# Sum of two tables and relu in one VectorE instruction: the first layer of a position bias

## The chip, the cores and the metric

The kernel runs on one core of one Trainium2 chip. The metric is the device time of one execution in microseconds (us). The engines are TensorE (PE in the profile; its weight loads are PEld), VectorE (DVE), ScalarE (ACT), GpSimd (POOL) and SyncE (SP). Executions of one kernel agreed within some 0.2% here.

## The reference, cut to what matters

The program is a sequence of four layers on an input of 2 x 512 x 32 x 32. The first is an attention with sampled keys whose scores get a bias from a small network of three layers on the distance of query and key:

```python
pos = grid_q[:, :, None, :] - grid_kv[:, None, :, :]
bias = jnp.sign(pos) * jnp.log1p(jnp.abs(pos))
bias = jax.nn.relu(bias @ cpb_w1 + cpb_b1)      # the layer that is changed
bias = jax.nn.relu(bias @ cpb_w2 + cpb_b2)
bias = (bias @ cpb_w3 + cpb_b3).reshape(...)
sim = jnp.einsum('bhid,bhjd->bhij', qh, kh) + bias
# ... softmax, values, projection, an MLP, and three more attention layers (cut)
```

The distance has an x part and a y part, so the first layer is the sum of one table over 32 columns and one over 32 rows, then a relu.

## The kernel before

A *unit* is one tile of 128 hidden channels by 1024 queries for one key. There are 1024 units. `first` makes the first layer on VectorE (in one unit of four, "quad 3", the relu is on ScalarE), `second` multiplies by the 128 x 128 weights on TensorE and evicts `z` from PSUM with ScalarE, `third` adds four units into `sim`.

```python
h1p = l0.enter_context(tc.tile_pool(name="att_h1", bufs=4))
ps_z = l0.enter_context(tc.tile_pool(name="att_ps_z", bufs=3, space=PSUM))
# ... (cut)
def first(u):
    # ... loads of the tables (cut)
    h1 = h1p.tile([P, H, W], F32, name="h1")
    nc.vector.tensor_tensor(                                       # L359
        h1,
        tx[:, quad, ri, :].unsqueeze(1).to_broadcast([P, H, W]),
        ty[:, quad, ri, :].unsqueeze(2).to_broadcast([P, H, W]),
        ALU.add,
    )
    h1f = h1.rearrange("p y x -> p (y x)")
    if quad == 3:
        nc.scalar.activation(h1f, h1f, AF.Relu)                    # L367
    else:
        nc.vector.tensor_scalar(h1f, h1f, 0.0, None, ALU.max)      # L369
    return h1f

def second(h1f):
    z = zt([P, HW], "z")
    for half in range(2):
        n = slice(half * HALF, (half + 1) * HALF)
        nc.tensor.matmul(z[:, n], cpb_w2, h1f[:, n], start=True, stop=True)   # L376
    h2 = h2p.tile([P, HW], F32, name="h2")
    nc.scalar.activation(h2, z, AF.Relu, bias=col("cpb_b2"))       # L378
    return h2
# ... (cut)
AHEAD = 2
for u in range(AHEAD):
    ready[u] = first(u)
for u in range(units + 2):
    if u + AHEAD < units:
        ready[u + AHEAD] = first(u + AHEAD)
    if u < units:
        h2s[u] = second(ready.pop(u))
    if u % 3 == 2:
        next(behind, None)      # one step of the work of other head pairs: offsets, samples, softmax
    # ... every eighth unit: third() for two rows, at the end of a head pair its scores (cut)
```

A step of `behind` on VectorE stands behind the sums of the units up to u + 2, and before all later ones.

## Time and profile before

| | before |
|---|---|
| median | 4073.86 us (4071.02 to 4075.19, 4 runs) |
| granted clock of TensorE | 0.991 |
| stage of the position bias | 84 to 2499 us of the span of 4073.9 |
| in that stage busy | TensorE 2371.6, VectorE 1910.8, ScalarE 1455.9 us |
| TensorE idle just before `z` | 43.4 us |

A group's line gives engine, operation, output<-input and the count, then busy time and the mean length of one, then the engine's idle time just before them and who ended it. The first thing to read is that TensorE is busy for 98% of the stage and VectorE for 79% (the weight loads, busy for 40%, 964 us, do not show how full TensorE is); the second is how little of TensorE's idle time stands before `z`. The lines themselves stand in the prediction below.

### The profile page before, as it was taken

How to read it: one execution, taken by the hardware profiler on the slowest of the kernel's cores; microseconds unless marked ns; L12 is line 12 of the kernel's file. 1: busy time of each engine (PE TensorE's matmuls, PEld its weight loads, DVE VectorE, ACT ScalarE, POOL GpSimd, SP SyncE). 2: the span in 40 equal slices, each digit the busy share in tenths (PEclk: the TensorE clock that was granted, in tenths of full speed). 3: DMA queues.
4: the chain of work that ended last, by engine and by line, in shares of the span. 5: the costliest groups of instructions: out<-in, count | busy, mean ns of one | idle time of the engine just before them, and what ended most of it. 6: DMA issues, size and time to landing. Idle time of an engine off the chain costs nothing.

```text
span 4073.9 us, 33014 instructions
## 1 busy us (share of the span) xinstructions
PE 3957.9 (97%) x13114; PEld 1627.1 (40%) x13114; DVE 2330.7 (57%) x2566; ACT 1767.5 (43%) x1843; POOL 264.5 (6%) x176
## 2 busy tenths in 40 slices
PE   6999999999999999999999998999999999999999
PEld 4343344343343343343343433444433333444443
DVE  3877877877877777877877774000016436230222
ACT  2665666665665466665656653111114324101011
POOL 0000110110010000010010010000000000000000
PEclk8999999999999999999999999999999999999999
DMA  3000101000011000000000000100010000000000
GB/s 110 21 16 11 22 16 54 20 16 16 16 16 16 11 16 16 16 21 11 22 16 13 19 16 0 52 8 11 8 49 1 1 0 1 13 0 0 0 21 22
DMA packets 95726, 72.87 MB, mean 18 GB/s; under 512 B 10576, under 2 KB 84688, under 8 KB 95056
## 3 DMA queue, kind: packets, MB, share of 16 engines
q1 hardware_dynamic: 92736, 69.18, 6.5%
q8 instruction: 108, 1.77, 0.2%
q10 hardware_dynamic: 2832, 1.51, 0.1%
q14 instruction: 50, 0.41, 0.0%
HBM read 62.03 MB, written 8.65 MB: 17 GB/s over the span
## 4 chain that ended last, share of the span: by engine, by line
PE 87%; DVE 10%; ACT 2%; issue 1%; DMA 0%; POOL 0%; ACTq 0%; SPq 0%; DVEq 0%; POOLq 0%
PE z L376 36%; PE sim L385 10%; PE pw L135 5%; PE ph L835 5%; PE pp L844 5%; PE pm L865 4%; DVE h L359 4%; PE pmv L135 4%; PE score L950 3%; PE pv L997 3%; PE score L135 3%; DVE acc L226 2%; DVE h L369 2%; PE pp L135 1%; PE ppr L890 1%
## 5 line engine op out<-in xcount | busy, mean ns | idle before, releaser
L376 PE MATMUL z<-h,cpb_w 128*128 128x512 f32 x4096 | 1818.8, 598 | 43.4 <-DVE h L369 28.3
L378 ACT ACTIVATE h<-z,pc 128x1024 f32<-128x1024 f32 x1024 | 1132.4, 1110 | 784.6 <-PE z L376 782.0
L359 DVE TENSOR_TENSOR h<-tab,tab 128x1024 f32<-128x1024 f32 x1024 | 1252.1, 1231 | 313.1 <-PE z L376 310.8
L376 PEld LDWEIGHTS z<-h,cpb_w 128*128 128x128 f32 x4096 | 760.8, 190 | 1065.4 <-issue 966.1
L369 DVE TENSOR_SCALAR h<-h 128x1024 f32<-128x1024 f32 x768 | 560.8, 730 | 26.3
L385 PE MATMUL sim<-h,w 128*32 128x512 f32 x4096 | 466.0, 595 | 0.0
L367 ACT ACTIVATE h<-h 128x1024 f32<-128x1024 f32 x256 | 269.3, 1052 | 131.7 <-DVE h L359 131.1
L345 POOL TENSOR_SCALAR tab<-tab,pc 128x512 f32<-128x512 f32 x64 | 120.4, 1882 | 2170.2 <-DMA tab<-slog_d 1469.3
L385 PEld LDWEIGHTS sim<-h,w 128*32 128x32 f32 x4096 | 120.2, 110 | 320.8 <-issue 320.2
L951 ACT ACTIVATE p<-score 128x1024 f32<-128x1024 f32 x144 | 139.5, 1020 | 212.4 <-PE score L950 210.0
L847 DVE SCALAR_TENSOR_TENSOR x<-pp,pc,x 128x512 f32<-128x512 f32 x16 | 12.0, 751 | 375.7 <-PE pp L844 375.7
L135 PE MATMUL pw<-p,vT 128*128 128x512 f32 x512 | 222.9, 597 | 1.3 <-DVE y L1049 1.3
L835 PE MATMUL ph<-xn,wa 128*128 128x512 f32 x512 | 220.9, 593 | 1.4 <-POOL xn L819 1.4
L844 PE MATMUL pp<-hid,wb 128*128 128x512 f32 x512 | 220.4, 592 | 0.0
L901 DVE TENSOR_TENSOR acc<-acc,p 128x2048 f32<-128x2048 f32 x56 | 129.7, 2316 | 133.2 <-ACT p L951 86.0
L838 ACT ACTIVATE hid<-ph,pc 128x512 f32<-128x512 f32 x64 | 44.0, 687 | 332.6 <-PE ph L835 332.6
L135 PEld LDWEIGHTS pw<-p,vT 128*128 128x128 f32 x512 | 97.8, 191 | 123.5 <-issue 122.0
L835 PEld LDWEIGHTS ph<-xn,wa 128*128 128x128 f32 x512 | 97.2, 190 | 123.1 <-issue 120.4
L844 PEld LDWEIGHTS pp<-hid,wb 128*128 128x128 f32 x512 | 97.4, 190 | 122.3 <-issue 122.3
L865 PE MATMUL pm<-hc,wa 128*128 128x512 f32 x256 | 128.5, 629 | 6.2 <-DMA wa<-in_qkv_w 6.2
L950 PE MATMUL score<-q,k 64*128 64x512 f32 x512 | 127.2, 615 | 0.0
L997 PE MATMUL pv<-p,vT 128*64 128x512 f32 x512 | 123.8, 605 | 0.0
(191 smaller groups left out, 1981.9 us busy)
## 6 DMA issues: line engine op xcount, KB each, us to landing
tab<-slog_d SPq DMA_DIRECT2D x128, 256.0 KB, 6.0
wa<-in_qkv_w SPq DMA_DIRECT2D x8, 768.0 KB, 7.4
x<-in_x SPq DMA_DIRECT2D x8, 512.0 KB, 5.2
xt<-in_xt SPq DMA_DIRECT2D x8, 512.0 KB, 4.0
wa<-in_mlp_w SPq DMA_DIRECT2D x4, 1024.0 KB, 15.8
wb<-in_mlp_w SPq DMA_DIRECT2D x16, 256.0 KB, 5.4
x_d<-x SPq DMA_DIRECT2D x16, 256.0 KB, 2.0
out<-x SPq DMA_DIRECT2D x16, 256.0 KB, 2.0
```

The costliest lines, as they stand in the source:

```text
L135: nc.tensor.matmul(pm, w, m, start=(k == 0), stop=(k == len(pairs) - 1))
L359: nc.vector.tensor_tensor(h1, tx[:, quad, ri, :].unsqueeze(1).to_broadcast([P, H, W]), ty[:, quad, ri, :].unsqueeze(2).to_broadcast([P, H, ...
L367: nc.scalar.activation(h1f, h1f, AF.Relu)
L369: nc.vector.tensor_scalar(h1f, h1f, 0.0, None, ALU.max)
L376: nc.tensor.matmul(z[:, n], cpb_w2, h1f[:, n], start=True, stop=True)
L378: nc.scalar.activation(h2, z, AF.Relu, bias=col("cpb_b2"))
L385: nc.tensor.matmul(sim[quad * 32 : quad * 32 + 32, n], w3[:, 31 - r : 63 - r], h2s[quad][:, n], start=(r == 0), stop=False,)
L835: nc.tensor.matmul(ph, w1[:, k, m * P : (m + 1) * P], xn_now[:, k, :], start=(k == 0), stop=(k == CC - 1))
L844: nc.tensor.matmul(pp, w2[:, k, m * P : (m + 1) * P], h1[:, k, :], start=(k == 0), stop=(k == HID // P - 1))
L865: nc.tensor.matmul(pm, w[:, k, cols], h[k][:, n], start=(k == 0), stop=(k == CC - 1))
L950: nc.tensor.matmul(sc[:, part, :], k[r, left[part]], q[r, n], start=True, stop=True)
L997: nc.tensor.matmul(pv[part * 64 : part * 64 + 64, n], vT[:, ls, lo : lo + 64], lp[:, part, n], start=(ls == 0), stop=(ls == 7),)
```

## The change

The two VectorE instructions become one custom instruction, `TENSOR_ADD_SAT`. By its definition in the library that the kernel imports it from it adds two inputs, takes the minimum with a first scalar and the maximum with a second. With the largest float and zero it is a sum and a relu. The intent is to spare 768 instructions on VectorE and 256 on ScalarE.

```diff
-            nc.vector.tensor_tensor(
-                h1,
-                tx[:, quad, ri, :].unsqueeze(1).to_broadcast([P, H, W]),
-                ty[:, quad, ri, :].unsqueeze(2).to_broadcast([P, H, W]),
-                ALU.add,
+
+            nc.vector._custom_dve(
+                TENSOR_ADD_SAT,
+                out=h1,
+                in0=tx[:, quad, ri, :].unsqueeze(1).to_broadcast([P, H, W]),
+                in1=ty[:, quad, ri, :].unsqueeze(2).to_broadcast([P, H, W]),
+                s0=float(np.finfo(np.float32).max),
+                s1=0.0,
             )
-            h1f = h1.rearrange("p y x -> p (y x)")
-            if quad == 3:
-                nc.scalar.activation(h1f, h1f, AF.Relu)
-            else:
-                nc.vector.tensor_scalar(h1f, h1f, 0.0, None, ALU.max)
-            return h1f
+            return h1.rearrange("p y x -> p (y x)")
```

(An import is cut.)

More of the change, by code (lines that the diff above doesn't have):

```diff
@@ L9 @@
 from concourse._compat import with_exitstack
+from concourse.dve_ops import TENSOR_ADD_SAT
 F32 = mybir.dt.float32
```

## The prediction

> **What bounds the kernel now.** I read the page first (busy shares, slices, chain of waits), then the waits of TensorE alone in the stage of the position bias, then the stage's timeline around those waits.
>
> ```profile
> PE 3957.9 (97%) x13114; PEld 1627.1 (40%) x13114; DVE 2330.7 (57%) x2566; ACT 1767.5 (43%) x1843; POOL 264.5 (6%) x176
> ...
> PE   6999999999999999999999998999999999999999
> DVE  3877877877877777877877774000016436230222
> PEclk8999999999999999999999999999999999999999
> ...
> L376 PE MATMUL z<-h,cpb_w 128*128 128x512 f32 x4096 | 1818.8, 598 | 43.4 <-DVE h L369 28.3
> L378 ACT ACTIVATE h<-z,pc 128x1024 f32<-128x1024 f32 x1024 | 1132.4, 1110 | 784.6 <-PE z L376 782.0
> L359 DVE TENSOR_TENSOR h<-tab,tab 128x1024 f32<-128x1024 f32 x1024 | 1252.1, 1231 | 313.1 <-PE z L376 310.8
> L369 DVE TENSOR_SCALAR h<-h 128x1024 f32<-128x1024 f32 x768 | 560.8, 730 | 26.3
> L367 ACT ACTIVATE h<-h 128x1024 f32<-128x1024 f32 x256 | 269.3, 1052 | 131.7 <-DVE h L359 131.1
> ```
>
> TensorE is busy nearly everywhere and its clock is full; VectorE is at seven to eight tenths in the first 25 slices and itself waits 310.8 us there for TensorE to give back a buffer. The changed lines (L359, L369, L367) lie in that stage alone, which runs from 84 to 2499 us. All that TensorE waits for in it:
>
> ```profile
> PE z L376 <- DVE h L369: 28.3, 24, 2.4
> PE z L376 <- ACT h L367: 9.6, 18, 1.4
> PE z L376 <- ACT h L378: 5.3, 5, 1.2
> ```
>
> That is 43.2 us in 47 waits. The chain of waits, in order of time, shows what an undisturbed stretch looks like:
>
> ```profile
> 311.03 13.93 PE z L376 x32
> 328.53 13.93 PE z L376 x32
> 346.03 13.93 PE z L376 x32
> ```
>
> One period of 8 units (32 passes of z and the sim passes between) takes 17.50 us with no wait. The stage has 1024 units, so 128 periods: 128 x 17.50 = 2240 us. The stage is 2499 - 84 = 2415 us. The other TensorE work in it (offsets, samples, scores, transposes, projection) has some 130 us by the busy column of its groups, and 2240 + 130 + 43 = 2413: the account closes, so outside those 47 waits TensorE is the bound and VectorE's speed buys nothing.
>
> A waiting matmul loses a little more than the idle time shown. A pass is recorded as 593 ns, but in a row passes start 429 ns apart (16 passes in 6.87 us), so a break also loses the overlap of some 0.16 us: 47 x 0.16 = 7.7 us. **The ceiling of the change is thus 43 + 8 = 51 us, 1.25% of 4072.8.**
>
> Where the waits come from is seen in the timeline at a change of head pair:
>
> ```profile
> 1286.53 1.22 DVE L415 TENSOR_REDUCE mx<-pt 128x16 f32<-128x1024 f32 x1 [6.91 <-PE pt L412]
> ...
> 1287.79 1.22 DVE L418 TENSOR_TENSOR at<-pt,mx 128x1024 f32<-128x1024 f32 x1
> 1288.93 1.22 DVE L359 TENSOR_TENSOR h<-tab,tab 128x1024 f32<-128x1024 f32 x1
> ...
> 1290.18 0.69 DVE L369 TENSOR_SCALAR h<-h 128x1024 f32<-128x1024 f32 x1
> ...
> 1291.02 1.96 PE L376 MATMUL z<-h,cpb_w 128*128 128x512 f32 x4 [1.09 <-DVE h L369]
> ```
>
> VectorE first has to wait for TensorE's transposes, then does two softmax operations, and only then makes the next unit; the two units made ahead are used up and TensorE stands for 1.09 us. The relu is the last 0.7 us ahead of the matmul.
>
> [...] No trace so far holds such a custom instruction[...].
>
> **The change part by part.**
> - VectorE: 1024 tensor_tensor (1252.1 us) become 1024 fused instructions[...]. 768 tensor_scalar (560.8 us) go. VectorE busy: 2331 - 561 = 1770 us, 43%. In a row an add and its relu take 1.86 us from start to start (1288.93 to 1290.79), an add alone 1.14 us (1287.79 to 1288.93); so a unit of three of the four quads costs VectorE 0.72 us less.
> - ScalarE: 256 relus (269.3 us) go: 1767 - 269 = 1498 us, 37%. The fourth quad also loses a hop from VectorE to ScalarE and its place in ScalarE's queue, where it stood between the evictions of z.
> - TensorE: the same matmuls, nothing added. No buffer, transfer or byte is changed.
> Most of the 830 us removed lies beside TensorE. What counts is each of the 47 waits, which I went through in the timeline, in four kinds:
> 1. Head-pair changes with the softmax on VectorE. Five of the seven show waits of about 1.1, 0.2 and 1.6 us, 14.6 us in all. After: the first unit is ready 0.7 us sooner, which leaves 0.36. For the later one, from 1288.93: three units 3 x 1.14, a sum 1.25, a reciprocal 0.29, a product 1.14, then the unit's own 1.25 and 0.12 for the signal: ready at 1296.4. TensorE would ask for it at about 1295.7; 0.7 us stay. About 1.0 of 2.9 us each: 5 us stay. The other two changes show one wait of 1.36 us on the ScalarE relu; 0.36 each stays, 0.7 in all.
> 2. The sample weights (a 1.15 us operation that waits for ScalarE): five waits, 6.7 us. Each is shortened by 0.7 to 0.8: 2.7 us stay.
> 3. The offset taps (six instructions, 2.16 us) and the small sample products: waits of 0.2 to 1.3 us. VectorE is behind there only because it had worked without a break for several units at 1.86 us each; at 1.14 it would have caught up. Nothing stays. The waits behind ScalarE's table loads (about 1 us) go with the 1.05 us relu that stood in the same queue.
> 4. The first unit of all: 2.40 us, of which 0.7 goes: 1.7 stays.
> Sum that stays: 5 + 0.7 + 2.7 + 1.7 = 10 us; I add 2 for waits that I can't foresee: 12. Saved idle: 43 - 12 = 31. Of the 47 breaks some 18 to 20 stay, so 27 to 29 times 0.16 us comes on top: 4.5. Saved in all about 36 us: **4072.8 - 36 = 4037 us, 0.9% faster.**
>
> **The rivals.**
> - A slow custom instruction. If the two further steps or the dispatch of the program cost time, VectorE loses the gain: the average unit now takes (3 x 1.86 + 1.14)/4 = 1.68 us of it, so at some 1.75 us per instruction the change is a wash on VectorE and only ScalarE's part is won (4050 to 4070). TensorE asks for a unit every 17.50/8 = 2.19 us; beyond 2.2 us an instruction, VectorE with its other work would be the bound, and a loss of 2% would come. [...] I take 5% for over 1.6 us.
> - TensorE is busy anyway and the waits move elsewhere: on ScalarE's evictions of z (three PSUM buffers), or on VectorE's softmax. The weight loads already wait 58.1 us for the evictions at L378, though hardly any of that reaches a matmul (5.3 us). If half the waits come back this way, the time is about 4055. Against it: ScalarE is at 6 tenths and loses a fifth of its work in the stage.
> - A large gain, read off the chain of waits, which gives VectorE 10% of the span (L359 4%, L369 2%), or off 830 us of removed work: 100 us or more, under 3970. Against it is the ceiling of 51 us; the chain walks through VectorE while TensorE is fed from units made ahead.
> - All waits go: 4022.
>
> **Range and chances.** The centre is 4037; the low end, 4024, is nearly the ceiling, the high end, 4054, the case of half the waits coming back or a somewhat slower instruction. Over 2% faster needs 81 us, above the ceiling: 1%. Over 2% slower needs the very slow instruction: 2%. Within 2%: 97%.
>
> **What would show it.** Right: the fused group at 1.2 to 1.25 us x1024, VectorE near 1770 and ScalarE near 1498 us busy, TensorE's idle before z at 8 to 16 us, its releaser mostly VectorE at head-pair changes and at the sample weights, the rest of the kernel from 2499 us on as long as before. Wrong: a fused instruction over 1.4 us; idle before z still over 25 us; a period of other than 17.50 us in undisturbed stretches; or a granted clock that falls when TensorE stands less.

The forecast's sum: it came to 31 + 4.5, about 36 us saved, and 4072.8 - 36 = 4037 us. The forecast takes the fused instruction to last as long as the add does in the trace before (median 1219 ns, starts 1.14 us apart); that was the assumption and no trace had shown it. The chance of 5% for over 1.6 us is an estimate without other support.

## The result, and the profile after

The changed kernel took 4034.27 us (4031.47 to 4037.9, 4 runs) against 4073.86. The ratio is 0.9904 with an interval of 0.9887 to 0.9921. The granted clock was 0.991 in the profiled run of either. The result was correct.

Of the page of the changed kernel: busy times, VectorE's slices, the groups of the stage. L361 is the fused instruction, L375 `z`, L377 its eviction.

```profile
PE 3949.7 (98%) x13114; PEld 1629.2 (40%) x13114; DVE 1809.8 (45%) x1798; ACT 1546.7 (38%) x1587; POOL 211.7 (5%) x176
...
DVE  2655655655655655655655552000016446130222
...
L375 PE MATMUL z<-h,cpb_w 128*128 128x512 f32 x4096 | 1810.3, 597 | 10.9 <-DVE h L361 10.3
L361 DVE CUSTOM_DVE_ANT_1 h<-tab,tab 128x1024 f32<-128x1024 f32 x1024 | 1242.9, 1230 | 784.9 <-PE z L375 784.1
L377 ACT ACTIVATE h<-z,pc 128x1024 f32<-128x1024 f32 x1024 | 1138.8, 1114 | 1095.6 <-PE z L375 1095.4
```

The fused instruction has a mean of 1230 ns, the add had 1231. VectorE now waits 784 us for TensorE to give back a buffer, against 311: it has nearly half a millisecond more to spare, and nearly all of it went into waiting. TensorE's idle time before `z` went from 43.4 to 10.9 us.

The stage in one window each, before and after (window, its length, then busy time of each engine with its count of instructions, granted clock, share of the DMA engines, GB/s):

```profile
84.00:2499.00 2415.00, 2371.63 (x8803) 964.10 (x8802) 1910.76 (x2166) 1455.85 (x1443) 216.67 (x124) 1.00 0.08 18
```

```profile
84.00:2458.00 2374.00, 2363.35 (x8803) 967.08 (x8804) 1390.98 (x1398) 1234.62 (x1186) 163.10 (x124) 1.00 0.08 18
```

The whole gain lies in this stage: what follows it took 1575 us before and 1576 after. In undisturbed stretches a period still takes 17.50 us, as the chain of waits of the changed kernel shows:

```profile
256.10 13.93 PE z L375 x32
270.03 3.57 PE sim L384 x32
273.60 13.93 PE z L375 x32
```

The waits that are left at a change of head pair, in the timeline of the changed kernel:

```profile
1267.60 1.23 DVE L417 TENSOR_TENSOR at<-pt,mx 128x1024 f32<-128x1024 f32 x1
1268.74 3.49 DVE L361 CUSTOM_DVE_ANT_1 h<-tab,tab 128x1024 f32<-128x1024 f32 x3
...
1270.10 5.39 PE L375 MATMUL z<-h,cpb_w 128*128 128x512 f32 x12 [0.36 <-DVE h L361]
...
1273.68 1.22 DVE L423 TENSOR_TENSOR at<-at,sm 128x1024 f32<-128x1024 f32 x1
...
1274.82 4.62 DVE L361 CUSTOM_DVE_ANT_1 h<-tab,tab 128x1024 f32<-128x1024 f32 x4
1276.19 1.95 PE L375 MATMUL z<-h,cpb_w 128*128 128x512 f32 x4 [0.70 <-DVE h L361]
```

The two waits of 0.36 and 0.70 us stand where the kernel before had 1.09, 0.18 and 1.70 (at 1291.02, 1293.15 and 1298.55 us of its trace): VectorE still does its softmax ahead of the next unit, but each unit comes 0.7 us sooner.

**A second way to count.** A pass of TensorE that comes a little late shows no idle time, because the recorded pass is longer (593 ns) than the distance to the next one (429), so a break loses up to some 0.16 us (593 - 429) that no idle column shows; before, 51 breaks are 50.4 us by starts and 43.4 us of idle time. So I also took the starts of the matmuls from the trace and summed what lies over 429 ns between a pass of `z` and the next pass of `z` (and the few breaks between side work and `z`). Over 170 ns I call it a break, from 20 to 170 ns a short delay.

| kernel | median us | ratio to before | idle before z | breaks: count, us | short delays, us |
|---|---|---|---|---|---|
| before | 4073.9 | 1 | 43.4 | 51, 50.4 | 20.8 |
| changed | 4034.3 | 0.9904 | 10.9 | 28, 15.1 | 15.5 |
| quads 0 to 2 fused | 4040.8 | 0.9916 | 16.7 | 31, 21.3 | 16.6 |
| quad 3 fused | 4068.0 | 0.9982 | 36.1 | 42, 42.6 | 19.5 |
| changed, 3 ahead | 4018.2 | 0.9860 | 2.0 | 6, 2.7 | 13.8 |
| before, 3 ahead | 4055.0 | 0.9950 | 23.0 | 48, 31.9 | 18.0 |
| quad 3 fused, 3 ahead | 4034.0 | 0.9904 | 14.4 | 20, 16.3 | 15.9 |
| a clamp more | 4102.1 | 1.0069 | 58.1 | 58, 68.8 | 24.9 |
| fused twice | 4381.4 | 1.0753 | 233.0 | 452, 319.6 | 44.2 |

From before to changed, breaks give 50.4 - 15.1 = 35.3 us and short delays 20.8 - 15.5 = 5.3, together 40.6 us; the profiled spans differ by 4073.9 - 4033.5 = 40.4. The time is accounted for. In most of these kernels 123 or 124 of the short delays are one of 0.104 us in nearly every period, 12.8 us in all, close behind the change from `sim` to `z`; the kernel with three ahead has hardly any other.

### The profile page after: what moved, and what is told of

Its sections match the earlier page's. It is cut to its first block, busy times and chain, and to the rows that moved or that the text cites. A ratio compares the mean times of both kernels' runs of the same rounds, so it can differ in the third digit from the quotient of the medians.

```text
span 4033.5 us, 33371 instructions
## 1 busy us (share of the span) xinstructions
PE 3949.7 (98%) x13114; PEld 1629.2 (40%) x13114; DVE 1809.8 (45%) x1798; ACT 1546.7 (38%) x1587; POOL 211.7 (5%) x176
## 4 chain that ended last, share of the span: by engine, by line
PE 96%; DVE 3%; ACT 1%; issue 0%; DMA 0%; POOL 0%; SPq 0%; DVEq 0%; ACTq 0%; POOLq 0%
PE z L375 42%; PE sim L384 11%; PE pw L136 5%; PE ph L834 5%; PE pp L843 5%; PE pm L864 4%; PE pmv L136 4%; PE score L949 3%; PE pv L996 3%; PE score L136 3%; PE pp L136 1%; PE ppr L889 1%; DVE h L361 1%; PE pk L136 1%; PE pm L1089 1%; PE pf L136 1%
## 5 line engine op out<-in xcount | busy, mean ns | idle before, releaser
L375 PE MATMUL z<-h,cpb_w 128*128 128x512 f32 x4096 | 1810.3, 597 | 10.9 <-DVE h L361 10.3
L361 DVE CUSTOM_DVE_ANT_1 h<-tab,tab 128x1024 f32<-128x1024 f32 x1024 | 1242.9, 1230 | 784.9 <-PE z L375 784.1
L377 ACT ACTIVATE h<-z,pc 128x1024 f32<-128x1024 f32 x1024 | 1138.8, 1114 | 1095.6 <-PE z L375 1095.4
L375 PEld LDWEIGHTS z<-h,cpb_w 128*128 128x128 f32 x4096 | 763.7, 190 | 1021.5 <-issue 986.5
L346 POOL TENSOR_SCALAR tab<-tab,pc 128x512 f32<-128x512 f32 x64 | 94.3, 1474 | 2155.1 <-DMA tab<-slog_d 1881.8
L136 PE MATMUL score<-t,hc 128*128 128x512 f32 x256 | 110.2, 592 | 0.0
L902 DVE TENSOR_TENSOR acc<-p 128x2048 f32<-128x2048 f32 x12 | 27.4, 2280 | 165.1 <-ACT p L1075 110.0
```

What stands on the lines that cost most here:

```text
L136: nc.tensor.matmul(pm, w, m, start=(k == 0), stop=(k == len(pairs) - 1))
L361: nc.vector._custom_dve(TENSOR_ADD_SAT, out=h1, in0=tx[:, quad, ri, :].unsqueeze(1).to_broadcast([P, H, W]), in1=ty[:, quad, ri, :].unsque ...
```

## The experiments

The theory: TensorE bounds the stage, and it loses time only where VectorE's side work delays the next unit past the units made ahead; the change shortens each such delay. The rivals: ScalarE's queue is what counts (the relu of quad 3 stands between the evictions); the fused instruction has a hidden cost; the units made ahead, not VectorE's amount of work, are the matter. "Before", in the same rounds as the first four runs, took 4074.44 us; as the next four (two with three units ahead, two with more work on VectorE) 4076.41; as the last three (the mark and two more with three ahead) 4073.86.

**The changed kernel again.** No edit.

> The changed kernel once more, as the mark for the three that share its chip. Both theories: ratio to before 0.990 to 0.991, some 4034 us, TensorE's idle before z near 11 us with some 18 waits on the fused instruction.

4034.19 us, ratio 0.9901 (0.9886 to 0.9916), idle before `z` 10.9 us with 18 waits on the fused instruction. The traces of two runs give the same waits.

**Only quads 0 to 2 fused.**

```diff
+            if quad == 3:
+                nc.vector.tensor_tensor(h1, tx..., ty..., ALU.add)      # shortened
+                nc.scalar.activation(h1..., h1..., AF.Relu)
+            else:
                 nc.vector._custom_dve(TENSOR_ADD_SAT, ...)
```

> Only the VectorE half of the change: quads 0 to 2 fused, quad 3 keeps its add on VectorE and its relu on ScalarE. My theory (VectorE late behind its softmax, weights and tap work is most of it): the 28.3 us of waits on the VectorE relu shrink to about 7, those on ScalarE's relu (9.6 us before) shrink by half because VectorE is earlier, ScalarE evictions stay at 5; idle before z 15 to 22 us, time 4045 to 4052. Rival (ScalarE's queue is the cause, the relu in it holds up the evictions of z): little won, over 4058. The short delays of weight loads behind ScalarE evictions (58.1 us in 81 waits before, 22.2 in 57 after) should stay above 45 us in either theory.

4040.76 us, ratio 0.9916 (0.9902 to 0.9929): 33.7 us won, more than expected. What TensorE waits for in the stage (engine, line, for whom, us in total, times, longest):

```profile
PE z L384 <- DVE h L370: 8.9, 17, 1.7
...
PE z L384 <- ACT h L368: 6.1, 8, 1.4
PE z L384 <- ACT h L386: 1.6, 2, 1.0
```

The idle time before `z`, 16.7 us, was in the range I had given. VectorE's waits were 8.9 us where I had said about 7, ScalarE's relu 6.1 where I had said half of 9.6, the evictions 1.6 where I had said 5 (the next run shows why). The weight loads' waits behind evictions fell from 58.1 to 29.7 us, which I had not expected: ScalarE has the same work here as before, so these waits follow VectorE's lateness, not ScalarE's load. Most of the fall is in waits that only bear the evictions' name: those that name the eviction of the unit just before, which is not needed (see the next run), made 24.6 us in the kernel before and make 0.8 here.

**Only quad 3 fused.**

```diff
+            if quad != 3:
+                nc.vector.tensor_tensor(h1, tx..., ty..., ALU.add)      # shortened
+                nc.vector.tensor_scalar(h1..., h1..., 0.0, None, ALU.max)
+            else:
                 nc.vector._custom_dve(TENSOR_ADD_SAT, ...)
```

> Only the ScalarE half: quad 3 fused, quads 0 to 2 keep add and relu on VectorE. My theory: the waits on the VectorE relu stay at 25 to 30 us, those on ScalarE's relu go or turn into waits on the fused instruction of some 3 us, evictions 0 to 1; time 4053 to 4062. Weight-load waits behind ScalarE evictions fall to 20 to 30 us, which would account for the 4 us by which the change gained more than I worked out (shorter delays than the overlap of two passes, which no idle time shows). Rival (ScalarE's queue is the main cause): under 4048.

4068.04 us, ratio 0.9982 (0.9969 to 0.9996): only 6.4 us won, less than either theory said.

```profile
PE z L384 <- DVE h L368: 29.6, 25, 2.4
...
PE z L384 <- ACT h L386: 5.3, 6, 1.2
...
PE z L384 <- DVE h L370: 1.0, 3, 0.4
```

The waits on the VectorE relu stay, as expected; those on ScalarE's relu are gone. The 5.3 us that the list puts down to evictions are not what they seem. The list names whatever came last, and in four of these six waits (1.24 us each, 5.0 in all) that is a bystander, as in the first of them:

```profile
509.33 1.11 ACT L386 ACTIVATE h<-z,pc 128x1024 f32<-128x1024 f32 x1 [0.60 <-PE z L384]
509.70 0.69 DVE L368 TENSOR_SCALAR h<-h 128x1024 f32<-128x1024 f32 x1
...
510.54 1.96 PE L384 MATMUL z<-h,cpb_w 128*128 128x512 f32 x4 [1.24 <-ACT h L386]
```

The eviction named is that of the unit just before. With three PSUM buffers a unit needs the eviction of the unit three before, and that one had ended 3.5 us earlier. The relu of the unit itself ended 0.15 us before the matmul, so the wait is VectorE's. The kernel before has three such waits (3.7 of its 5.3 us). So the evictions hold TensorE for 0.3 us here, as expected, and for 1.6 in the kernel before; VectorE's waits went from 32.0 us (28.3 + 3.7) to 35.6 (29.6 + 1.0 + 5.0), which took back part of what ScalarE's relu had cost. The weight loads' waits stayed at 61.7 us and the short delays at 19.5: my thought that ScalarE's relief makes the extra 4 us is refuted. The two halves add up, 33.7 + 6.4 = 40.1 against 40.2 for both, and five sixths of the gain is VectorE's half. The rival that ScalarE's queue is the main cause falls.

**No relu at all.** Its output is wrong, which doesn't matter for the time.

```diff
-            nc.vector._custom_dve(TENSOR_ADD_SAT, ...)
+            nc.vector.tensor_tensor(h1, tx..., ty..., ALU.add)           # shortened
```

> Wrong result on purpose: the plain add, no relu of the first layer anywhere. It does the changed kernel's work without the two further steps of the fused instruction. If the fused instruction costs what an add costs: same time as the changed kernel within 0.1% (4030 to 4038), instruction mean 1225 to 1235 ns, same waits. If dispatch or the further steps cost something hidden: over 4 us faster than the changed kernel.

4034.19 us, the same as the changed kernel on the same chip to the last digit, and the same waits:

```profile
L373 PE MATMUL z<-h,cpb_w 128*128 128x512 f32 x4096 | 1810.3, 597 | 10.9 <-DVE h L361 10.3
L361 DVE TENSOR_TENSOR h<-tab,tab 128x1024 f32<-128x1024 f32 x1024 | 1243.6, 1230 | 783.6 <-PE z L373 782.7
```

The relu inside the fused instruction costs nothing that can be measured. (The comparison with the reference called this result correct, so it does not see the missing relu; why it does not was not looked into. The fused form's correctness is therefore carried by its definition, not by this test.)

**Three units ahead**, with and without the change. The four buffers are kept; the third unit ahead reuses the buffer of unit u - 1.

```diff
-        AHEAD = 2
+        AHEAD = 3
```

> The changed kernel with three units made ahead in VectorE's program order instead of two, the same four buffers. My theory (the 10 us of waits that stay are VectorE's softmax and sample-weight work, placed before the next unit when only two are in hand): a third unit gives TensorE 1.71 us more, so waits of 0.36 to 0.70 us all go; only the first unit's 1.7 us stays; with 18 breaks less, 11 us won: 4021 to 4027, idle before z 2 to 4 us. Rival (the wait moves: the fourth buffer is freed too late, VectorE's side work comes later and stops TensorE's transposes or products instead): 4030 or more, with new waits at the products or transposes.

> The kernel before with three units ahead, unfused. If the lost time was a matter of how far ahead VectorE is, not of how much it has to do, this wins most of what the fused instruction won: 4040 to 4050, waits on the VectorE relu under 10 us. If VectorE's amount of work is the cause (it never gets far enough ahead to use the third unit, being busy 80% of the stage), under 10 us are won: over 4062.

Fused: 4018.16 us, ratio 0.9860 (0.9844 to 0.9875), faster than expected. Idle before `z` is 2.0 us, of which the first unit has 1.7:

```profile
L375 PE MATMUL z<-h,cpb_w 128*128 128x512 f32 x4096 | 1805.1, 596 | 2.0 <-DVE h L361 1.7
```

Unfused: 4055.0 us, ratio 0.9950 (0.9936 to 0.9963), between the two expectations. The waits on VectorE's relu nearly went (2.9 us), and others came in their place. The two lines of its waits, and the timeline around the longest one:

```profile
PE z L376 <- ACT h L378: 19.3, 22, 2.3
...
PE z L376 <- DVE h L369: 2.9, 3, 2.4
```

```profile
1060.29 1.06 ACT L367 ACTIVATE h<-h 128x1024 f32<-128x1024 f32 x1 [4.20 <-DVE h L359]
1061.25 3.11 ACT L378 ACTIVATE h<-z,pc 128x1024 f32<-128x1024 f32 x3
...
1062.40 3.97 PE L376 MATMUL z<-h,cpb_w 128*128 128x512 f32 x5 [2.31 <-ACT h L378]
```

ScalarE stood idle for 4.20 us because the next instruction in its queue, the relu of quad 3, waited for VectorE's add; the evictions of `z` stood behind it, and then three came in a row. Here the named evictions are the right ones: in 18 of the 22 waits it is that of the unit three before, 0.05 us ahead of the matmul, and in the other four a tile of side work had taken a buffer in between. The reading was tested:

**Three ahead, only quad 3 fused**, together with the fused kernel of three ahead once more as the mark.

> The fused kernel with three units ahead once more, as the mark for the two that share its chip: ratio to before 0.985 to 0.987.

> Three units ahead, and only quad 3 fused; quads 0 to 2 keep add and relu on VectorE. In the unfused kernel with three ahead TensorE waited 19.3 us for ScalarE's evictions of z, which stood in the queue behind a relu that waited for VectorE's add. If that order is the cause, the fused instruction in quad 3 alone removes it: evictions under 3 us of waits, idle before z 4 to 10 us, time 4022 to 4034, near the kernel with everything fused, though VectorE has as much to do as before. If instead VectorE's amount of work is what delays the evictions, over 4042, with the waits back on VectorE's relu.

The mark: 4018.0 us, ratio 0.9864. Quad 3 alone: 4033.97 us, ratio 0.9904 (0.9887 to 0.9920).

```profile
PE z L384 <- DVE h L368: 13.2, 12, 2.4
...
PE z L384 <- ACT h L386: 0.3, 2, 0.2
```

The waits for evictions fell from 19.3 to 0.3 us by taking the relu out of ScalarE's queue: the relu there was the cause. In 15 of the 22 waits (14.7 us) ScalarE had stood idle in front of such a relu, for 0.9 to 4.2 us, which is the order's doing. In the other seven (4.6 us) it had not; there the relu's own 1.05 us of work, which this edit removes too, may have been enough, and no run separates the two. But 13.2 us came back on VectorE's relu, so the amount of work on VectorE matters too; idle before `z` was 14.4 us where I had said 4 to 10, and the time was at the upper end of the 4022 to 4034 expected.

**Three ahead, evictions in halves.**

```diff
-            nc.scalar.activation(h2, z, AF.Relu, bias=col("cpb_b2"))
+            for half in range(2):
+                n = slice(half * HALF, (half + 1) * HALF)
+                nc.scalar.activation(h2[:, n], z[:, n], AF.Relu, bias=col("cpb_b2"))
```

> Fused, three ahead, and ScalarE's eviction of z in two halves, so that a half is read as soon as its own passes are done. If evictions of z still cost TensorE something, up to 10 us are won (under 4012). If the stage is at TensorE's floor (17.50 us a period, all short delays left are the one of 0.10 us at each change from sim to z), nothing is won: within 4 us of the mark, or slower by the doubled fixed cost on ScalarE.

4021.42 us, ratio 0.9872, some 3 us slower than the mark: earlier evictions buy nothing more. (The fixed cost on ScalarE that the expectation speaks of shows in the trace of the kernel before: at 548.44 us an activation of 128x128 takes 0.37 us, the next, an eviction of 128x1024, 1.11. By these two the part that does not grow with the length is an estimated 0.26 us. That it made the 3 us was not shown.) Together with the 17.50 us period and the 2.7 us of breaks this says that the fused kernel with three ahead has the stage close to what TensorE needs for these matmuls in this order. What is left is the short delay of 0.104 us in each period, whose cause no run sought. The fused kernel with three ahead is the fastest version, 0.4% below the changed kernel.

**More work on VectorE: a clamp more, and the fused instruction twice.** Results unchanged.

```diff
             nc.vector._custom_dve(TENSOR_ADD_SAT, out=h1, ...)
+            nc.vector.tensor_scalar(h1, h1, 0.0, None, ALU.max)          # one kernel
+            nc.vector._custom_dve(TENSOR_ADD_SAT, out=h1, ...)           # the other kernel
```

> The changed kernel with a needless second clamp on VectorE after each fused instruction, in place, result unchanged: 1.86 us of VectorE per unit in all four quads (before: 1.68 on average), no relu on ScalarE. My theory: TensorE still asks for a unit every 2.19 us only, so it bounds, but VectorE is later than in the kernel before: waits on VectorE 40 to 60 us, time 4060 to 4090. Rival (VectorE's total is what counts, 1 us lost per us added): 1024 x 0.72 = 737 us lost, over 4700.

> The changed kernel with each fused instruction issued twice: 2.28 us of VectorE per unit against the 2.19 us at which TensorE asks for one. My theory: here VectorE becomes the bound of the stage: 1024 x 2.28 = 2335 us and its other work of some 150 us, 2485 against a stage of 2374 now: 110 to 140 us longer, 4145 to 4180. If it stays under 4100, VectorE has more slack than worked out.

A clamp more: 4102.11 us, ratio 1.0069 (1.0053 to 1.0084). The waits on VectorE were as expected: 47.8 us by name, and 10.0 of the 10.3 us that the list puts down to evictions (eight waits of the kind shown for quad 3, with the relu replaced by the clamp). The time was not, because the overlap lost in 30 more breaks (about 5 us, estimated at 0.16 each) and 24.9 - 15.5 = 9.4 us more of short delays came on top. The 737 us that a loss of one for one would make are far off. Twice: 4381.42 us, ratio 1.0753 (1.0737 to 1.0770), 200 us over what I expected. Its timeline on VectorE (L361 the first, L369 the second of a unit):

```profile
605.54 1.22 DVE L361 CUSTOM_DVE_ANT_1 h<-tab,tab 128x1024 f32<-128x1024 f32 x1
606.79 1.22 DVE L369 CUSTOM_DVE_ANT_1 h<-tab,tab 128x1024 f32<-128x1024 f32 x1
...
607.93 1.22 DVE L361 CUSTOM_DVE_ANT_1 h<-tab,tab 128x1024 f32<-128x1024 f32 x1
```

The second of a unit writes the same buffer and starts 1.25 us after the first; the next unit starts 1.14 after that. A unit takes 2.39 us, not the 2.28 I had used: 1024 x 2.39 = 2447 us. The kernel before shows what else VectorE does in the stage, 1910.8 us busy less 1024 x 1.68 for its units, some 190. That is 2637 of the 2714 us of this stage (VectorE busy 2612); most of the rest is VectorE's own waits, which now cost in full. VectorE is the bound here, as the theory said, but I had mis-sized it.

By VectorE's time per unit (1.14, 1.68, 1.86 and 2.39 us) the kernels without ScalarE's relu and with two ahead took 4034, 4068, 4102 and 4381 us. Each us added to all 1024 units cost some 63 us from 1.14 to 1.68, 190 from 1.68 to 1.86 and 530 from 1.86 to 2.39, where a loss of one for one would be 1024. So the curve is not flat below TensorE's 2.19 us: it steepens well before VectorE's time reaches them, and VectorE's side work (some 190 us) comes on top of these times.

## Why the prediction was right

The prediction was 4037 us; the median was 4034.3, inside the range of 4024 to 4054 and, as forecast, within 2%. The saving was 39.6 us where 36 was forecast; the forecast's base of 4072.8 us lies 1.1 under the median before.

- *The bound and the ceiling.* Right. All was won in the stage, the period stayed at 17.50 us, and removing 830 us of busy time from two engines gave 40. The ceiling of 51 us was a little low: the unseen short delays, 20.8 - 12.8 = 8 us beyond those that every period has, were not in it. With three ahead, the change and the order together won 56 to 58 us (4073.86 to 4018.0, and 4076.41 to 4018.16 in the other rounds). That the account closed to 2 us (2413 against 2415) was in part luck: it left out these 8 us and the 8 of lost overlap, and the 130 us for other work were about as much too large. The same sum for the changed kernel, 2240 + 130 + 11 = 2381 us, is 7 over its stage of 2374.
- *The fused instruction as long as the add.* Right: median 1225 ns (the add's 1219), and the kernel without a relu, 4034.19 us like the changed one, shows no hidden cost. In the prediction this was an assumption; the runs settled it.
- *Busy times.* VectorE 1809.8 us where I had said 1770, ScalarE 1546.7 where I had said 1498. I took the groups' busy time off the engine's, but records of instructions in a row overlap (1.22 us long, starts 1.14 apart on VectorE) and the engine's busy time counts an overlap once, so less disappears than the sum of the group.
- *What stays of the 47 waits.* Right nearly to the digit: 0.36 and about 0.7 us at head-pair changes (measured 0.36 and 0.69 to 0.70), 1.7 at the start (1.67), 2.7 in all at the five sample weights (2.6); the sum 10.6 us in 20 waits where I had said 12, with 2 for the unforeseen, in 18 to 20. I had gone by the timeline there: three of the five waits at the sample weights are among the 5.3 us that the list gives to evictions, and I had counted them, rightly, as VectorE's. Waits and breaks together, 31 + 4.5 = 35.5 us, came out at 35.3.
- *The term that was missing:* short delays inside the overlap of two passes, 5.3 us. I had looked for them at ScalarE; the kernel with quad 3 alone fused refuted that (19.5 us of short delays) and the one with quads 0 to 2 alone got most of them (16.6). In these runs they follow VectorE's lateness.
- *The rivals.* "Waits that move" did not happen in the changed kernel but did in the kernel before with three ahead, at the evictions I had named, though for a reason I had not: a queue held by an instruction that waits for another engine. "A wash at some 1.75 us an instruction, 4050 to 4070" was too kind: between 1.68 us (4068) and 1.86 us (4102) it would be some 4080, read off the two.

## What to carry to other kernels

When one engine is the bound, list its waits one by one and ask how much of each goes: that list, not the busy time removed, is the size of the gain. An engine that is not full (here VectorE, busy for 79% of the stage) still costs where its side work stands ahead of the next piece of the main work; less work for it and one more piece made ahead both helped (39.6 and 21.4 us), and they were worth most together (58). An instruction that waits for another engine, put into the queue that frees the buffers, can turn that engine's lateness into a stop of the bound (14.7 us in 15 waits here). And a releaser that a list names can be a bystander: count the buffers and see whether the wait could be for it at all.
